# Seven products of quarters in the input projections of a state-space layer, and decay by rows

## The chip, the cores and the metric

The kernel runs on one core of a Trainium2 chip, as one launch. The metric is the device time of that core in microseconds (us), from the kernel's start to its end. Each kernel is run several times; the number to compare is the median. A profile comes from one further execution, whose time differs a little from the median.

## The reference

The model is a small stack on 1024 tokens of width 512: a mixture of experts, attention with 32 heads, the experts again, a linear layer with low-rank experts, a state-space (Mamba-2) layer, and the low-rank layer again. The change touches only the state-space layer. Cut to what matters, with `u` the normalized input (1024 x 512):

```python
proj = u @ in_proj_w.T                       # gate 4096, x 4096, B 1024, C 1024, dt 64
xBC  = silu(conv(hbc))                       # causal, 4 taps per column, plus a bias
dt_p = softplus(dt + dt_bias);  dA = exp(dt_p * A)
# 64 heads of 64 columns, 8 groups of 8 heads that share B and C (128 wide each)
state = state * dA_t + dtx_t * B_t           # per head 64 x 128, token by token
y_t   = state . C_t
y     = y + x * D
yn    = y * rsqrt(mean(y*y over the group) + EPS) * norm_weight * silu(gate)
out   = yn @ out_proj_w.T
```

Here `u @ in_proj_w.T` is the projection. The recurrence is computed in chunks of 128 tokens. Inside a chunk, y is a matrix product with a lower-triangular matrix of decays; what came before the chunk enters through the state at the chunk's start, decayed by a factor that depends on head and token alone.

## The kernel before, in words

All operands are fp32. Tokens lie on 8 tiles of 128. `hT` holds the normalized input transposed: 4 blocks of 128 rows, 1024 columns.

The function `mamba` walks over 16 **units**: 8 groups of heads, each in two halves of 512 tokens. A unit has 4 chunks of 128 tokens, and 5 **pairs** of projected blocks of 128 columns: pair 0 is B and C, pairs 1 and 2 are x, pairs 3 and 4 are the gate. For each chunk, the loop at the end of `mamba` calls `scan` for the running unit, `project_pair` for the next unit (two pairs in the first chunk, one in each other), `prepare` for the next chunk, and `project_out` for this one. A list scheduler in the framework then fixes the order in which the instructions stand on each engine; each engine works its own queue in that order, and semaphores join them. In the built program before the change, the order on TensorE is close to the written one.

- **`project_pair`** fills two PSUM banks (`ps_in`, pool `pbig`) through `project`: for each of two blocks, 4 matmuls of 128x512 (L230). For B, C and x, `conv_silu` then lets ScalarE read the bank with scale and bias (L1157), VectorE add three shifted taps from the same bank (L1161) and, in the second half, patch the first columns from `hist`, the last three columns of the first half (L1170). A Silu follows (L1180). `xd` is x scaled by D for a whole unit (L1224). For the gate, one Silu reads both banks (L1204).
- **`prepare`** loads two rows of decays per head from DRAM, each spread over 128 partitions (`dd`, SyncE's queue, L1259). VectorE turns the first into the triangular matrix `e` (L1265, L1273), and GpSimd multiplies the second with C into `cs` (L1290). Transposes (`ps_tr`, L156) and VectorE give `xdt` (L1278); GpSimd gives `xw` (L1284).
- **`scan`** computes y in one bank (`ps_y`, L1308): 8 matmuls of `xdt` with `e`, 8 of the old state with `cs`. VectorE adds `xd` (L1317), ScalarE squares (L1321), VectorE multiplies with the gate (L1323), and GpSimd adds four blocks of squares in two steps (L1340, L1341). `ps_st` (L1326) and two additions carry the state on (L1333, L1336).
- **`project_out`** sums the squares over partitions (`ps_ss`, L1349), gets the root on VectorE and GpSimd (L149, L150), multiplies with the output weights (`ps_out`, L1360) and adds to `x` (L1363).
- **`load_group`** loads four weight tiles per group on SyncE's queue, into the four buffers of `wpool`, and scales the output weights on ScalarE (L1146).

Other stages already use seven products: `products`, called at L884 and L912, and `sums` (L636), which builds the sums of weights on GpSimd.

## Time and profile before

| What | Value |
|---|---|
| median of 3 runs | 2933.5 us (2931.63 to 2933.84) |
| the profiled execution's own time | 2935.3 us |
| its span, first to last instruction | 2933.6 us |
| TensorE busy (PE) | 2800.9 us, 95% |
| VectorE busy (DVE) | 1745.8 us, 60% |
| ScalarE busy (ACT) | 709.4 us, 24% |
| GpSimd busy (POOL) | 898.8 us, 31% |
| mean granted TensorE clock | 0.978 |

PE is TensorE, PEld its weight loads, which overlap with matmuls; DVE is VectorE, ACT ScalarE, POOL GpSimd, SP SyncE. A line such as L230 is a line of the kernel's file, often that of a helper that many callers share, so the names of the tiles (`ps_in<-hT,w_x`) say which use is meant. A fp32 matmul shows as two passes, so a count of 512 stands for 256 calls. Buffers' numbers are left out of names.

### The profile page before, as it was taken

To read this page: it belongs to the slowest core of one execution; us is meant where nothing else is said; L and a number is where in the kernel's file an instruction comes from. 1 tells how busy PE (TensorE), PEld (TensorE's weight loads), DVE (VectorE), ACT (ScalarE), POOL (GpSimd) and SP (SyncE) were. 2 spreads that over 40 slices of the span, in tenths; PEclk is the share of its full clock that TensorE was granted. 3 is DMA by queue.
4 is the path that set the end of the run, shared out by engine and by line. 5 is a ranking of instruction groups with operands and counts; after the bars stand their busy time and mean duration, and the time that the engine had idled before them with its cause. 6 is when DMAs were issued, how large, how long until landed. Compare 5 with 4: busy or idle time off the path is not lost.

```text
span 2933.6 us, 30294 instructions
## 1 busy us (share of the span) xinstructions
PE 2800.9 (95%) x11051; PEld 1587.3 (54%) x11051; DVE 1745.8 (60%) x3239; ACT 709.4 (24%) x1381; POOL 898.8 (31%) x733
## 2 busy tenths in 40 slices
PE   5979999999999999999999769899999999999989
PEld 3435666656666666666654334454555555555544
DVE  3146555665656656556564234777776777767673
ACT  1212212231212222212222222422222232222320
POOL 4231112121122212112100230255554545455450
PEclk8989999999999999999999889999999999999999
DMA  8420001010010001001015340233232222223210
GB/s 297 126 72 29 15 15 44 1 44 15 15 44 15 29 15 43 15 15 43 1 36 194 101 122 18 83 101 108 86 108 94 86 98 97 93 87 122 87 44 29
DMA packets 102178, 196.99 MB, mean 67 GB/s; under 512 B 9040, under 2 KB 34800, under 8 KB 102032
## 3 DMA queue, kind: packets, MB, share of 16 engines
q1 hardware_dynamic: 84896, 157.15, 16.1%
q0 software_dynamic: 6240, 20.45, 2.7%
q10 hardware_dynamic: 10896, 17.47, 1.6%
q8 instruction: 89, 1.46, 0.2%
q14 instruction: 57, 0.47, 0.1%
HBM read 176.17 MB, written 18.87 MB: 66 GB/s over the span
## 4 chain that ended last, share of the span: by engine, by line
PE 84%; DVE 6%; POOL 4%; issue 3%; DMA 2%; ACT 0%; POOLq 0%; DVEq 0%; SPq 0%; ACTq 0%
PE ps_in L230 15%; PE ps_m L912 13%; PE ps_o L732 8%; PE ps_s L708 8%; PE ps_tr L156 7%; PE ps_out L1360 6%; PE ps_m L884 6%; PE ps_wo L821 6%; PE ps_e L510 5%; PE ps_y L1308 3%; PE ps_up L241 2%; PE ps_st L1326 1%; DVE xc L1161 1%; DVE e_seg L1265 1%; PE ps_v L241 1%
## 5 line engine op out<-in xcount | busy, mean ns | idle before, releaser
L708 PE MATMUL ps_s<-kT,qT 128*128 128x512 f32 (+3 forms) x768 | 292.8, 488 | 0.1
L732 PE MATMUL ps_o<-pT,v 128*128 128x512 f32 (+3 forms) x768 | 260.4, 489 | 0.0
L753 ACT COPY pT<-ps_tr 128x256 f32<-128x256 f32 (+2 forms) x192 | 91.7, 478 | 647.3 <-PE ps_tr L156 635.5
L722 ACT ACTIVATE pr<-ps_s,nm 128x128 f32<-128x128 f32 (+7 forms) x256 | 190.3, 744 | 238.3 <-DVE nm L719 207.9
L1360 PE MATMUL ps_out<-w_out,yg 128*128 128x512 f32 x512 | 241.1, 615 | 3.0 <-DVE yg L1323 3.0
L230 PE MATMUL ps_in<-hT,w_g 128*128 128x512 f32 x512 | 227.1, 596 | 8.2 <-issue 8.2
L1290 POOL TENSOR_TENSOR cs<-cT,dd 128x1024 f32<-128x1024 f32 x56 | 184.2, 3289 | 161.6 <-PE ps_y L1308 138.8
L230 PE MATMUL ps_in<-hT,w_x 128*128 128x512 f32 x512 | 225.8, 593 | 0.0
L732 PEld LDWEIGHTS ps_o<-pT,v 128*128 128x128 f32 x768 | 144.3, 191 | 145.6 <-issue 99.9
L719 DVE TENSOR_REDUCE nm<-ps_s 128x1 f32<-128x128 f32 (+7 forms) x256 | 192.2, 752 | 3.9
L156 PEld LDWEIGHTS ps_tr<-ident,pr 128*128 128x128 f32 x1152 | 136.9, 142 | 76.1 <-issue 44.8
L156 PE MATMUL ps_tr<-ident,pr 128*128 128x128 f32 x1152 | 171.4, 276 | 4.5 <-DVE pr L724 3.2
L510 PE MATMUL ps_e<-w_all,xt_s 128*128 (+1 forms) x368 | 168.1, 601 | 0.0
L724 DVE TENSOR_SCALAR pr<-pr,sm 128x128 f32<-128x128 f32 (+7 forms) x256 | 162.9, 637 | 7.7 <-DVE sm L723 0.5
L230 PEld LDWEIGHTS ps_in<-hT,w_g 128*128 128x128 f32 x512 | 96.6, 190 | 127.8 <-issue 127.8
L230 PEld LDWEIGHTS ps_in<-hT,w_x 128*128 128x128 f32 x512 | 97.0, 190 | 120.9 <-issue 120.4
L1265 DVE TENSOR_TENSOR_SCAN e_seg<-dd,eye 128x1024 f32<-128x1024 f32 x64 | 152.3, 2380 | 7.7 <-PE ps_y L1308 5.8
L1161 DVE SCALAR_TENSOR_TENSOR xc<-ps_in,conv,xc 128x511 f32<-128x511 f32 (+2 forms) x192 | 141.5, 737 | 17.9 <-ACT xc L1157 17.6
L708 PEld LDWEIGHTS ps_s<-kT,qT 128*128 128x128 f32 x768 | 127.5, 192 | 39.8 <-issue 26.8
L1360 PEld LDWEIGHTS ps_out<-w_out,yg 128*128 128x128 f32 x512 | 94.5, 195 | 98.4 <-issue 98.4
L806 POOL TENSOR_TENSOR so<-oT 128x256 f32<-128x256 f32 x28 | 20.0, 726 | 380.2 <-DVE oT L739 336.7
L1284 POOL TENSOR_TENSOR xw<-xdt,erev 128x512 f32<-128x512 f32 x56 | 58.4, 1043 | 251.6 <-DVE xdt L1278 195.0
(271 smaller groups left out, 4759.2 us busy)
## 6 DMA issues: line engine op xcount, KB each, us to landing
dd<-decay SPq DMA_DIRECT2D x128, 512.0 KB
w_all<-in_w_e_dram SPq DMA_DIRECT2D x16, 1024.0 KB
outs<-y_e ACTq DMA_DIRECT2D x46, 256.0 KB
w_v<-in_wkv_dram SPq DMA_DIRECT2D x8, 1024.0 KB
w_q<-in_wq_dram SPq DMA_DIRECT2D x32, 256.0 KB
w_k<-in_wkv_dram SPq DMA_DIRECT2D x8, 1024.0 KB
w_o<-in_wo_dram SPq DMA_DIRECT2D x8, 1024.0 KB
w_x<-in_in_wt_dram SPq DMA_DIRECT2D x8, 1024.0 KB
```

Source lines behind the costliest of these rows:

```text
L156: nc.tensor.transpose(ps[:, i * P : (i + 1) * P], src(i), ident)
L230: nc.tensor.matmul(ps[:, cols : cols + n], lhsT=w[:, k, c0 : c0 + P], rhs=hT[:, k, t0 : t0 + n], start=(k == 0), stop=(k == KT - 1),)
L510: nc.tensor.matmul(ps, lhsT=xt[:, k, :], rhs=w_all[:, bass.ds(ep, 1), k, :].rearrange("p e c -> p (e c)"), start=(k == 0), stop=(k == KT - 1),
L708: nc.tensor.matmul(ps[:, j : j + m], lhsT=qT[:, qt * P : (qt + 1) * P], rhs=kT[:, j : j + m], start=True, stop=True,)
L719: nc.vector.tensor_reduce(nm, ps[:, :n], AX.X, ALU.max, negate=True)
L722: nc.scalar.activation(pr[:, :n], ps[:, :n], AF.Exp, bias=nm, accum_out=sm)
L732: nc.tensor.matmul(ps[:, lo:512], lhsT=v[:, kb, hh * P : (hh + 1) * P], rhs=pT[:, kb, lo:512], start=(kb == 0), stop=(kb == last),)
L821: nc.tensor.matmul(ps[:, j, :], lhsT=lf[i][k][:, j * P : (j + 1) * P], rhs=rt[i][:, k, :], start=(first and j == 0 and k == 0), stop=(k == 1),
L912: nc.tensor.matmul(ps, lhsT=gr["left"][i][:, k, hh * P : (hh + 1) * P], rhs=right[i][:, k, :], start=(first and k == 0), stop=(last and k ...
L1265: nc.vector.tensor_tensor_scan(e.rearrange("p h l -> p (h l)"), dd[:, 0, :], eye8.rearrange("p h l -> p (h l)"), 0.0, ALU.mult, ALU.add,)
L1290: nc.gpsimd.tensor_tensor(cs, un["cT"][:, tok].unsqueeze(1).to_broadcast([P, HPG, P]), dd[:, 1, :].rearrange("p (h l) -> p h l", l=P), ALU ...
L1360: nc.tensor.matmul(po, lhsT=yg[:, k, :], rhs=w_o[:, k, :], start=(k == 0), stop=(k == 3))
```

## The change

It has four parts.

- **Projections as seven products.** Weights and input are cut into quarters (rows and columns halved). `quarter` makes four differences of `hT`'s quarters once per half on VectorE, one of them in place. `left_bc` and `left_in` make four sums of the weights' quarters per weight tile on GpSimd, one in place. `project_pair` becomes a generator with four steps: bank `pa` collects products 1, 6, 7 and 4, and ScalarE copies its content out (`snap`) before each next one; `pb` holds product 2 and `pc` products 5 and 3, in a second bank. VectorE adds three of the four results, ScalarE copies the fourth.
- **The convolution reads SBUF.** Results go to `raw`, which has three columns of history in front; the three taps are then full width, and the patches from `hist` are gone. `conv_both` runs one chunk later.
- **State's part of y decayed by rows.** `ps_z` is the old state times C: 4 matmuls of 128x128. VectorE multiplies it with the decays `ec`, which are loaded onto the two halves of the partitions; GpSimd adds `xd`; y is then `ps_y` plus that. `cs` is gone. `xd` is made per chunk, 4 pieces of 128 columns.
- **Buffers and loads.** `dd` is turned into `e` in place; `xdt`, `xw`, `xd`, `z`, `y`, `sq` and `yg` have one buffer each. The four weight loads of a group are spread over the chunks of two units.

The diff, cut to its core:

```diff
+                def quarter(hf):
+
+                    q1, q2 = (slice(hf * 512 + i * 256, hf * 512 + (i + 1) * 256) for i in range(2))
+                    b11, b12 = hT[:, :2, q1], hT[:, :2, q2]
+                    b21, b22 = hT[:, 2:, q1], hT[:, 2:, q2]
+                    t1, t2, t4 = (tt[:, hf, i, :, :] for i in range(3))
+                    nc.vector.tensor_tensor(t1, b12, b11, ALU.subtract)
+                    nc.vector.tensor_tensor(t2, b22, t1, ALU.subtract)
+                    nc.vector.tensor_tensor(t4, b21, t2, ALU.subtract)
+                    nc.vector.tensor_tensor(b12, b22, b12, ALU.subtract)
+                    quarters.append({1: b11, 2: b21, 3: b22, 4: t4, 5: t1, 6: t2, 7: b12})
...
+            def left_in(gr, n):
+                w, ss = gr["w_" + n], par.sums[n]
+                gr["l_" + n] = sums(
...
+            def conv_silu(raw, ct, dst):
...
                 for s in (1, 2, 3):
                     nc.vector.scalar_tensor_tensor(
-                        dst[:, s:],
-                        ps[:, : half - s],
+                        dst,
+                        raw[:, 3 - s : 3 - s + half],
...
+            def project_pair(un, j, convs):
...
+                snap = sn.tile([P, 4, n], F32, tag="snap", name="snap")
+                mm(pa, 1, True)
+                nc.scalar.copy(snap[:, 0, :], pa)
+                mm(pb, 2, True)
+                yield
+                mm(pa, 6)
+                nc.scalar.copy(snap[:, 1, :], pa)
+                mm(pc, 5)
+                nc.scalar.copy(snap[:, 3, :], pc)
+                yield
...
+                mm(pa, 7)
+                nc.scalar.copy(snap[:, 2, :], pa)
+                nc.vector.tensor_tensor(d1[:, :n], pb, snap[:, 0, :], ALU.add)
+                nc.vector.tensor_tensor(d2[:, n:], snap[:, 3, :], snap[:, 2, :], ALU.add)
+                yield
+                mm(pc, 3)
+                nc.vector.tensor_tensor(d1[:, n:], pc, snap[:, 1, :], ALU.add)
+                mm(pa, 4)
+                if gate:
+                    nc.scalar.activation(d2[:, n:], d2[:, n:], AF.Silu)
+                    nc.scalar.activation(d2[:, :n], pa, AF.Silu)
+                    nc.scalar.activation(d1, d1, AF.Silu)
                     return
+                nc.scalar.copy(d2[:, :n], pa)
...
+                e = ep.tile([P, HPG, P], F32, tag="dd", name="dd")
+                dd = e.rearrange("p h l -> p (h l)")
...
+                xd = w1.tile([P, 4, P], F32, tag="xd", name="xd")
+                for k in range(4):
+                    nc.scalar.activation(
+                        xd[:, k, :],
+                        un["xc"][:, k, tok],
...
-                    cs = ep.tile([P, HPG, P], F32, tag="cs", name="cs")
...
+                    pz = psml.tile([P, 512], F32, tag="ps", name="ps_z")
+                    for k in range(4):
                         nc.tensor.matmul(
+                            pz[:, k * P : (k + 1) * P],
+                            lhsT=before[:, k * P : (k + 1) * P],
+                            rhs=un["cT"][:, tok],
...
+                    z = w1.tile([P, 4, P], F32, tag="z", name="z_m")
+                    nc.vector.tensor_tensor(
+                        z, pz.rearrange("p (k l) -> p k l", l=P), ec, ALU.mult
+                    )
+                    nc.gpsimd.tensor_tensor(z, z, more, ALU.add)
+                    more = z
...
                 for i in range(4):
+                    pairs, early = [], convs
+                    convs = []
+                    if nxt is not None:
+                        pairs = [project_pair(nxt, j, convs) for j in plan[i]]
+                    go_on(pairs)
                     done = scan(un, i, *ready)
-                    if nxt is not None:
-                        for j in plan[i]:
-                            project_pair(nxt, j)
-                        if i == 1:
-                            finish_bc(nxt)
+                    go_on(pairs)
+                    for f in early:
+                        f()
...
+                    go_on(pairs)
+                    if un["gr"].pop("scale_o", False):
+                        scale_o(un["gr"])
                     project_out(*done)
+                    go_on(pairs)
```

## The prediction

> **What bounds the kernel now.** I first read the page's chain of work that ended last, to see which engine sets the end.
>
> ```profile
> PE 84%; DVE 6%; POOL 4%; issue 3%; DMA 2%; ACT 0%; POOLq 0%; DVEq 0%; SPq 0%; ACTq 0%
> PE ps_in L230 15%; PE ps_m L912 13%; PE ps_o L732 8%; PE ps_s L708 8%; PE ps_tr L156 7%; PE ps_out L1360 6%; PE ps_m L884 6%; PE ps_wo L821 6%; PE ps_e L510 5%; PE ps_y L1308 3%; PE ps_up L241 2%; PE ps_st L1326 1%; DVE xc L1161 1%; DVE e_seg L1265 1%; PE ps_v L241 1%
> ```
>
> TensorE sets it, and the products that the change rewrites (ps_in, L230) are its largest single piece. Next the busy time by stretch (columns: stretch, its length, then busy us of PE, PEld, DVE, ACT, POOL, then the granted clock).
>
> ```profile
> 1840.00:1860.00 20.00, 11.79 (x26) 5.67 (x26) 18.40 (x27) 12.51 (x16) 6.77 (x2) 0.83 0.39 135
> 2308.00:2376.00 68.00, 68.00 (x320) 35.72 (x315) 48.51 (x61) 16.17 (x24) 35.55 (x23) 1.00 0.23 78
> ```
>
> In the state-space stage (from 1876 us to about 2840 us) TensorE is busy for all 68.00 of 68 us: it waits for nobody. DVE has 29% free, POOL 48%. So the stage is as long as its matmuls, and a cut there counts in full, but every wait put on TensorE counts in full too. The first line, from the lead-in, shows a clock of 0.83 where TensorE idled (L230 after one idle of 8.2 us). Then one chunk in order of time (columns: start, duration, engine, line).
>
> ```profile
> 2230.37 1.09 PE L1308 MATMUL ps_y<-e_seg,xdt 128*64 128x128 f32 x16
> 2231.30 1.04 PE L1308 MATMUL ps_y<-cs,state 128*64 128x128 f32 x16
> 2232.27 1.13 PE L1326 MATMUL ps_st<-xw,btok 128*128 128x512 f32 x2
> 2233.23 7.03 PE L230 MATMUL ps_in<-hT,w_g 128*128 128x512 f32 x16
> 2234.72 0.68 DVE L1317 TENSOR_TENSOR y_m<-ps_y,xd 128x512 f32<-128x512 f32 x1
> 2235.49 0.63 ACT L1321 ACTIVATE sq<-y_m 128x512 f32<-128x512 f32 x1 [4.36 <-DVE y_m L1317]
> 2236.27 1.18 POOL L1340 TENSOR_TENSOR sq<-sq 128x256 f32<-128x256 f32 x1
> 2237.38 1.21 DVE L1273 TENSOR_TENSOR e_seg<-e_seg,gt 128x1024 f32<-128x1024 f32 x1
> 2237.53 1.38 POOL L1341 TENSOR_TENSOR sq<-sq 128x128 f32<-128x128 f32 x1
> 2240.10 0.60 PE L156 MATMUL ps_tr<-ident,xc 128*128 128x128 f32 x4
> 2240.54 0.28 PE L1349 MATMUL ps_ss<-ones,sq 128*128 128x1 f32 x2
> 2240.68 3.68 PE L1360 MATMUL ps_out<-w_out,yg 128*128 128x512 f32 x8
> 2244.29 1.09 PE L1308 MATMUL ps_y<-e_seg,xdt 128*64 128x128 f32 x16
> ```
>
> This is the cover that decides the case. ps_y is complete at 2232.3; the sum of squares needs it through y_m, sq and two POOL additions, which end at 2238.9; TensorE asks for it (ps_ss) at 2240.5. The 6.87 us of ps_in between them hide the whole chain, with 1.6 us to spare. The chunk takes 2244.29 - 2230.37 = 13.92 us. The chain of waits repeats every 127.2 us (POOL ss L150 at 2041.04 and 2168.19): two units of four chunks.
>
> **The change, part by part.**
>
> *Projections.* A fp32 matmul runs as two passes. Now: 16 passes of 512 columns take 6.87 us, 0.43 each. After: 7 products x 2 halves x 2 passes = 28 passes of 256 columns. The attention stage has such passes:
>
> ```profile
> 1378.81 1.89 PE L884 MATMUL ps_m<-w_v,tt 128*128 128x256 f32 x8
> 1380.53 1.89 PE L884 MATMUL ps_m<-sv,tt 128*128 128x256 f32 x8
> ```
>
> Eight start within 1.72 us: 0.216 each, so 28 take 6.04. Saved: 0.83 x 80 pairs = 66 us.
>
> *State's part of y.* Sixteen half-width passes (2231.30 to 2232.27, 0.97 us) become eight of 128x128; the eight ps_bc passes take 0.89. Saved: 0.08 x 56 = 4 us. With both, TensorE's work falls by 70 us: about 118 us per two units, if nothing waits.
>
> *ACT.* Added: 240 snapshots and 48 raw copies of 128x256 at 0.37 (pT of that shape), 107 us; the gate's one Silu (1.02) becomes three (about 1.5), 15; xd in 256 pieces of 128 columns, for which no row exists: between 0.27 (a plain copy, 128 columns) and 0.40 (that plus the 0.14 by which the scaled 512-column xd, 0.72, exceeds a plain copy, 0.58); I take 0.40, its own kind, so 102 for 46. About +180 us on an engine that is 24% busy: hidden as busy time. As a queue it isn't, see below.
>
> *DVE.* Goes: 144 patches from history (48 us) and the hist copies (7). Comes: 240 additions of 128x256 at about 0.39 (94), 56 z products at 0.68 (38), eight quarter differences (5). Net +82 us, within DVE's free 29%.
>
> *POOL.* Goes: cs, 184 us. Comes: z += xd, 56 x 1.27 = 71, and the weight sums, per group eight of 128x512 at 1.27 and four of 128x256 at 0.73 = 13.1, times 8 = 105. Busy time even; but cs was work that nobody waited for soon, and its replacements stand in TensorE's way.
>
> *SP and DMA.* 128 broadcasts of 512 KB become 64, and 112 of 128 KB. DVE's wait for dd was 1.9 us in all, so nothing is gained. SP issues 48 more, at 0.42. dd is now overwritten in place and its next load waits for ps_y of two chunks back, a chunk ahead of its use: about zero, at most a few us. The weight loads are spread over two units; w_out still lands some 5.6 us after its issue, then ACT scales it: hidden behind the first chunk's products as now.
>
> *The waits added, which decide.* In the order in which the changed program's instructions stand, three things are new.
>
> (a) ps_ss. After the last ps_z TensorE has ps_st (0.96), a transpose group (0.44) and 12, 6, 6 or 8 calls of 0.43 (plus ps_bc and bT, 1.3, in the third chunk): 6.6, 4.0, 5.3, 4.9 us. The chain is z 0.68, POOL add 1.27, y 0.68, sq 0.63, POOL 0.72 and 0.45 at their shortest, 4.8 with six hand-overs of 0.06; at mean durations (1.63 and 0.96 for the last two) 6.2. The old cover was 8.3 us for a chain of two links fewer.
>
> (b) POOL's queue. z_m's addition stands behind four sums of w_bc (2.9 us) once a group, and the sq addition amid four sums of w_x (5.1 us) and of w_g.
>
> (c) ACT's queue. xd now has one buffer, so its first piece waits until POOL has added the old one to z; behind it stand the snapshots for which the collecting bank, and so TensorE, waits. A worked chunk, from its first ps_y: ps_z ends at 3.2, z at 4.1, POOL is at the w_bc sums until 6.6, a short memset, the addition ends 8.05, xd takes ACT to 8.4, the snapshot ends at 8.8, and TensorE, idle since 5.7, goes on at 9.0 with its weights loaded: 3.2 us lost. y then ends at 8.8, sq at 9.7, POOL at 11.6, ps_ss comes at 11.7 instead of 10.3: 1.4 lost.
>
> I laid eight chunks out so, each instruction starting when its engine is free and its releaser done, durations from rows. Lost on products / on ps_ss, in us: 3.5/1.0, 4.3/1.4, 0.7/3.3, 5.3/3.3, 1.8/6.7, 1.3/1.4, 2.1/0, 1.7/3.2. That is 20.7 + 20.3 = 41 us per two units: 118 + 41 = 159 against 127.2. The same layout of the old order gives 126, so it is not biased against waits.
>
> *A rule against the change.* Rows first (shortest/median/longest, ns):
>
> ```profile
> L1323 DVE TENSOR_TENSOR yg<-y_m,sg x64: 674/991/1525, 1880.6 to 2895.6; 128x512 f32<-128x512 f32 x64
> L1161 DVE SCALAR_TENSOR_TENSOR xc<-ps_in,conv,xc x192: 648/736/750, 1842.4 to 2805.1; 128x511 f32<-128x511 f32 x64, 128x510 f32<-128x510 f32 x64, 128x509 f32<-128x509 f32 x64
> L1340 POOL TENSOR_TENSOR sq<-sq x60: 722/1702/2707, 1879.3 to 2824.3; 128x256 f32<-128x256 f32 x60
> ```
>
> The Trainium skill (SBUF — State Buffer, Who interferes with whom) says that a DVE instruction with two SBUF inputs and a GpSimd instruction that reads SBUF exclude each other for a whole instruction, while one SBUF input is free of it. The rows agree: yg (two SBUF inputs) and sq stretch, the convolution (PSUM and SBUF) doesn't; above, the second POOL addition ends with e_seg's 1.21. The change makes all 288 convolution steps read raw from SBUF. By rows at their shortest (0.65 instead of 0.74) that gains 26 us of DVE and the layout loses only 26 us per two units; by the rule, which stretches POOL's part of (a) and (b), 41. I take four fifths of the way to the rule.
>
> *Sum.* 15 units with projections, 7.5 pairs of units. By the rule 7.5 x 32 = 238, without it 7.5 x (118 + 26 - 127) = 130; at four fifths 216. Another page of the Trainium skill, TensorE: Matmul & The Clock Gate (Why this matters for your kernels), warns of idle gaps over about 3 us, after which the clock falls to half; around the 8.2 us gap the first stretch above lost 0.17 x 20 = 3.4 us of clock. Only the 6.7 us gap (once per two units) is likely to: by the layout's row zero, by the rule up to 25; I take 6. Lead-in and tail even out: the first products start before POOL has its sums, and the last unit has none. So +222 on the profiled execution's 2935.3 (span 2933.6 and 1.7 around it); the median of the runs, 2933.5, lies 1.8 lower. 3155.
>
> **The rivals.**
>
> *The waits bite, the port hardly does* (25%): 2933.5 + 130 = 3064. For it: cs, the longest POOL partner (3.29 us), is gone. Against: its place is taken by sums of 1.27, and the DVE steps with two SBUF inputs more than double (192 now, 288 + 80 added).
>
> *Worse* (12%): the clock falls in most long gaps and POOL's sums stretch each other: 3155 + 25 + 60 = 3240.
>
> *Faster* (5%): other work fills the waits. TensorE's place for it is the product of the next pair, put between. It would be 2933.5 - 70 = 2864. It decides if the loss stays under 70/15 = 4.7 us a unit, 1.2 a chunk; the worked chunk loses 4.6, and (a) alone, at shortest durations, 0.8 in the second chunk. I see nothing in the rows that shortens the two POOL links.
>
> *The products don't get cheaper* (3%): 28 passes equal 16 at 0.245 each; the row says 0.216. It adds up to 66 us.
>
> **How the numbers follow.** The case worked out has 55%: 3155, own range 3100 to 3215. With the others, the 8-in-10 range is 3040 to 3240; below it lie "faster" and the mildest of the first rival, above it half of "worse". Within 0.2% (6 us, about what a measurement can tell from no change): 1%. Faster 5%, slower 94%.
>
> **What would show it.** TensorE's busy share in the stage falls from 100% to 75-80%, with ps_ss waiting on POOL sq some 60 to 150 us in all and ps_in waiting on ACT snap and DVE; two units take near 155 us; ps_in's busy time falls by some 60 us; ACT's wait of xd on POOL z_m is among the longest; the convolution's DVE steps spread instead of sitting at 0.74. It is wrong if two units take under 127 us, or if TensorE's waits come mainly from a DMA.

## The result, and the profile after

The changed kernel takes 3191.7 us (median, 3187.92 to 3198.01) against 2933.7 us for the kernel before on the same chip: the ratio is 1.0884, with a 95% interval of 1.0869 to 1.0899. It is 258 us slower. The prediction was 3155 (range 3040 to 3240).

First the chain of work that ended last, of the changed kernel's page.

```profile
PE 73%; POOL 12%; DVE 8%; DMA 3%; issue 3%; ACT 1%; SPq 0%; POOLq 0%; DVEq 0%; ACTq 0%
PE ps_m L914 12%; PE ps_in L1268 9%; PE ps_o L734 8%; PE ps_s L710 7%; PE ps_out L1479 6%; PE ps_m L886 5%; PE ps_wo L823 5%; PE ps_tr L156 5%; PE ps_e L510 4%; PE ps_y L1410 2%; POOL z_m L1433 2%; PE ps_up L241 2%; POOL sq L1459 2%; PE ps_z L1422 2%; DVE xc L1233 1%
```

TensorE's share of the chain fell from 84% to 73%, and GpSimd's rose from 4% to 12%: `z_m` and `sq`, two additions on GpSimd, now stand in the chain themselves. Next the busy time by stretch (columns as before the change: stretch, its length, busy us of PE, PEld, DVE, ACT, POOL, granted clock, DMA share, GB/s).

```profile
2228.70:2389.83 161.13, 137.59 (x615) 91.30 (x614) 106.68 (x140) 55.86 (x140) 71.68 (x63) 0.94 0.20 61
2246.00:2251.20 5.20, 5.20 (x10) 2.20 (x10) 5.17 (x5) 0.46 (x2) 5.20 (x3) 0.67 0.01 3
```

The first line is two units: 161.13 us where they took 127.2, with TensorE idle for 23.5 of them and a granted clock of 0.94 where it was 1.00. The second is explained below. Then one chunk in order of time (start, duration, engine, line, with the idle time before it and its releaser in brackets).

```profile
2237.08 1.16 PE L1422 MATMUL ps_z<-cT,state 128*128 128x128 f32 x8
...
2238.31 0.68 DVE L1430 TENSOR_TENSOR z_m<-ps_z,ec 128x512 f32<-128x512 f32 x1
...
2239.14 1.27 POOL L1433 TENSOR_TENSOR z_m<-z_m,xd 128x512 f32<-128x512 f32 x1 [6.65 <-DVE z_m L1430]
...
2240.45 0.69 DVE L1436 TENSOR_TENSOR y_m<-ps_y,z_m 128x512 f32<-128x512 f32 x1 [0.62 <-POOL z_m L1433]
2241.22 0.63 ACT L1440 ACTIVATE sq<-y_m 128x512 f32<-128x512 f32 x1
...
2242.20 0.95 POOL L1459 TENSOR_TENSOR sq<-sq 128x256 f32<-128x256 f32 x1
...
2242.72 1.03 PE L1268 MATMUL ps_in<-hT,w_g 128*128 128x256 f32 x4
2243.12 1.71 POOL L638 TENSOR_TENSOR s_x<-w_x 128x512 f32<-128x512 f32 x1
...
2244.79 0.90 POOL L1460 TENSOR_TENSOR sq<-sq 128x128 f32<-128x128 f32 x1
...
2245.74 0.38 PE L1468 MATMUL ps_ss<-ones,sq 128*128 128x1 f32 x2 [1.99 <-POOL sq L1460]
2245.99 5.38 PE L1479 MATMUL ps_out<-w_out,yg 128*128 128x512 f32 x8
```

The chain that the prediction named is there link by link, with one of the sums of weights (`s_x`) between GpSimd's two additions of squares. It ends 1.99 us after TensorE has nothing left to do. And then the next work, the same eight passes of `ps_out` that took 3.68 us in the kernel before, takes 5.38: that is the stretch with the granted clock of 0.67. Such a wait is paid twice, once as idle time and once as a clock at half speed afterwards. The waits of the changed kernel (engine, line waited for: us in total, times, longest) name the same places:

```profile
ACT xd L1388 <- POOL z_m L1433: 151.4, 48, 6.4
PEld ps_ss L1468 <- POOL sq L1460: 135.3, 52, 5.8
PE ps_ss L1468 <- POOL sq L1460: 114.9, 43, 5.4
POOL raw L1297 <- DVE bT L1233: 96.9, 8, 22.5
PE ps_in L1268 <- ACT snap L1283: 33.0, 37, 2.2
```

**A ledger of TensorE.** For every kernel I took 48 chunks of the stage, from the fifth to the fifty-third start of `ps_out`, in the view in order of time, and split the time of two units into three: *idle* (TensorE had nothing to start), *clock* (half of the working time inside stretches at half clock, since passes that start 0.43 us apart elsewhere start 0.85 apart in them), and *work* (the rest: from the start of one group of passes to the start of the next, at full clock).

| us in two units | total | idle at ps_ss | idle at ps_in | clock | work |
|---|---|---|---|---|---|
| before | 127.1 | 0.6 | 0 | 0 | 126.5 |
| changed | 162.3 | 16.0 | 7.8 | 10.2 | 128.3 |

The difference, 35.2 us, times the 7.5 pairs of units is 264 us, against 258 measured, so the whole loss lies in this stage. The last column is the surprise: TensorE's own work did not get less at all. In the changed kernel 280 passes of `ps_in` take 66.7 us at full clock, 0.238 each, where 160 took 68.8; 128 passes of `ps_y` take 11.4 us, 0.089 each instead of 0.060, and 56 of `ps_z` take 7.0. Four rows of the chunk above show where the price comes from:

```profile
2235.22 1.13 PE L1268 MATMUL ps_in<-tt_m,w_x 128*128 128x256 f32 x4
2236.28 0.87 PE L1410 MATMUL ps_y<-dd,xdt 128*64 128x128 f32 x10
...
2238.94 1.03 PE L1268 MATMUL ps_in<-tt_m,s_g 128*128 128x256 f32 x4
2239.80 0.60 PE L156 MATMUL ps_tr<-ident,bT 128*128 128x128 f32 x4
```

From the start of one row to the start of the next, four passes between two groups of `ps_y` take 1.06 us, four in front of a transpose 0.86, which is 0.216 each. Over the 48 chunks, at full clock, each of 102 passes in front of `ps_y` takes 0.31 us to the next start, and each of the 54 that start right behind it takes 0.32; the 78 in front of transposes, `ps_z` and `ps_out` take 0.216. Of the 6.2 us that 280 passes take above 0.216 each, 2.6 lie beside `ps_y` and 3.2 beside a wait.

### The profile page after: what moved, and what is told of

It reads as the page before. It is cut to its first block, busy times and chain, and to the rows that moved or that the text cites. A ratio compares the mean times of both kernels' runs of the same rounds, so it can differ in the third digit from the quotient of the medians.

```text
span 3190.0 us, 32210 instructions
## 1 busy us (share of the span) xinstructions
PE 2883.1 (90%) x11563; PEld 1795.4 (56%) x11563; DVE 1855.6 (58%) x3351; ACT 875.6 (27%) x2095; POOL 949.1 (30%) x877
## 3 DMA queue, kind: packets, MB, share of 16 engines
q1 hardware_dynamic: 106144, 138.28, 13.4%
## 4 chain that ended last, share of the span: by engine, by line
PE 73%; POOL 12%; DVE 8%; DMA 3%; issue 3%; ACT 1%; SPq 0%; POOLq 0%; DVEq 0%; ACTq 0%
PE ps_m L914 12%; PE ps_in L1268 9%; PE ps_o L734 8%; PE ps_s L710 7%; PE ps_out L1479 6%; PE ps_m L886 5%; PE ps_wo L823 5%; PE ps_tr L156 5%; PE ps_e L510 4%; PE ps_y L1410 2%; POOL z_m L1433 2%; PE ps_up L241 2%; POOL sq L1459 2%; PE ps_z L1422 2%; DVE xc L1233 1%
## 5 line engine op out<-in xcount | busy, mean ns | idle before, releaser
L1479 PE MATMUL ps_out<-w_out,yg 128*128 128x512 f32 x512 | 302.6, 739 | 0.0
L1370 DVE TENSOR_TENSOR_SCAN dd<-dd,eye 128x1024 f32<-128x1024 f32 x64 | 181.3, 2833 | 13.3 <-DMA dd<-decay 13.2
L1479 PEld LDWEIGHTS ps_out<-w_out,yg 128*128 128x128 f32 x512 | 116.8, 240 | 121.8 <-issue 120.7
L1433 POOL TENSOR_TENSOR z_m<-z_m,xd 128x512 f32<-128x512 f32 x56 | 73.7, 1315 | 354.4 <-DVE z_m L1430 278.6
L1233 DVE SCALAR_TENSOR_TENSOR xc<-raw,conv,xc 128x512 f32<-128x512 f32 x192 | 164.1, 856 | 14.3 <-ACT xc L1225 13.0
L710 PEld LDWEIGHTS ps_s<-kT,qT 128*128 128x128 f32 x768 | 127.5, 192 | 39.8 <-issue 26.8
L1468 PE MATMUL ps_ss<-ones,sq 128*128 128x1 f32 x152 | 30.5, 281 | 127.3 <-POOL sq L1460 114.9
L1388 ACT ACTIVATE xd<-xc,dsk 128x128 f32<-128x128 f32 x256 | 93.0, 396 | 152.5 <-POOL z_m L1433 151.4
L661 POOL TENSOR_SCALAR w_q<-w_q 128x1024 f32<-128x1024 f32 x16 | 44.3, 2770 | 289.2 <-DMA w_q<-in_wq_dram 288.6
L518 DVE TENSOR_TENSOR y_e<-ps_e,b_all 128x512 f32<-128x512 f32 x46 | 31.8, 692 | 169.0 <-PE ps_e L510 165.5
L1482 DVE SCALAR_TENSOR_TENSOR x<-ps_out,ss,x 128x512 f32<-128x512 f32 x64 | 47.8, 746 | 136.1 <-PE ps_out L1479 119.1
```

The lines of the kernel that those rows point to most:

```text
L710: nc.tensor.matmul(ps[:, j : j + m], lhsT=qT[:, qt * P : (qt + 1) * P], rhs=kT[:, j : j + m], start=True, stop=True,)
L1233: nc.vector.scalar_tensor_tensor(dst, raw[:, 3 - s : 3 - s + half], conv[:, ct, 3 - s : 4 - s], dst, ALU.mult, ALU.add,)
L1370: nc.vector.tensor_tensor_scan(dd, dd, eye8.rearrange("p h l -> p (h l)"), 0.0, ALU.mult, ALU.add,)
L1479: nc.tensor.matmul(po, lhsT=yg[:, k, :], rhs=w_o[:, k, :], start=(k == 0), stop=(k == 3))
```

## The experiments

All times are medians; ratios are against the kernel before on the same chip, with 95% intervals. The ledger's lines are worked out in the same way for each.

**The two parts of the change apart.** The first run makes only the second part of the change, in the kernel before:

```diff
-                terms = [(xdt, e)] + ([(before, cs)] if before is not None else [])
...
+                more = un["xd"][:, :, tok]
+                if before is not None:
+                    pz = psml.tile([P, 512], F32, tag="ps", name="ps_z")
...
+                    nc.gpsimd.tensor_tensor(z, z, more, ALU.add)
```

> The kernel before with one part of the change alone: the state's part of y decayed by rows (ps_z, ec, z on VectorE, its addition of xd on GpSimd), cs gone, the projections as before. Theory of the waits in order: the projections of 6.9 us still stand between ps_y and ps_ss, and they covered the old chain with 1.6 us to spare; the new one is 2.1 us longer, so the cover is short by some 0.5 us in a chunk at mean durations: TensorE's work is even (ps_z's eight passes take 1.0 us, as much as the sixteen that go), and the time rises by 0 to 28 us: about 2945. Rival, in which the two parts of the change cost alike: above 3000. Rival, in which cs was what stretched VectorE's and GpSimd's instructions: below 2930.

Measured: 2944.3 us, ratio 1.0035 (1.0022 to 1.0048), as the theory of the waits said. Two units take 127.5, with 126.7 of work and 0.8 of idle time. Its waits at `ps_ss`:

```profile
PE ps_ss L1363 <- ACT sq L1335: 12.6, 4, 3.8
PE ps_ss L1363 <- POOL sq L1355: 6.7, 9, 0.8
```

So the longer chain alone hardly ever shows: 6.7 us in all on GpSimd's additions. The first line is the last unit, which has no products to stand between. The run also shows that the decay by rows saves TensorE nothing: in two units the 56 passes of `ps_z` take 7.0 us, and `ps_y` falls by 6.1 (14.3 to 8.2).

The second run is the changed kernel with that part put back:

```diff
+                terms = [(xdt, e)] + ([(before, cs)] if before is not None else [])
...
-                    z = w1.tile([P, 4, P], F32, tag="z", name="z_m")
...
-                    nc.gpsimd.tensor_tensor(z, z, more, ALU.add)
```

> The changed kernel with the state's part put back: cs on GpSimd again (made in place in its own load), sixteen passes of cs with the state collected into ps_y, y is ps_y plus xd; no ps_z, no z. The seven products stay. Theory of the waits in order: the chain before ps_ss loses z and GpSimd's addition (2.1 us), and xd no longer waits for GpSimd; but cs (2.3 us and up) stands in GpSimd's queue again, amid the sums of the weights. The waits that ACT's snapshots and VectorE's additions put on ps_in stay, as do most gaps in front of ps_ss: 3120 to 3185, about 3160. Rival, in which the parts simply add up: 3192 less what the rows alone add to the kernel before, so 3165 to 3192. Rival, in which the decay by rows is the main cause: below 3020.

Measured: 3112.3 us, ratio 1.0613 (1.0595 to 1.0630). This is below what I expected; the parts do not add up. The decay by rows costs 11 us alone, and 79 us (3191.7 less 3112.3) when it stands beside the rest of the change. The ledger: 125.0 of work, 7.7 idle at `ps_ss`, 12.9 at `ps_in`, 6.4 of clock. What is shorter is the wait at `ps_ss`, whose chain lost two links; at `ps_in` TensorE waits more than in the changed kernel.

**The place of the products.** The change also spreads a pair's products over four places of the chunk, ahead of `scan`, behind it, behind `prepare` and behind `project_out`, where the old kernel had all of them behind `scan`. One run takes that alone into the kernel before:

```diff
+                    go_on(pairs)
                     done = scan(un, i, *ready)
-                    if nxt is not None:
-                        for j in plan[i]:
-                            project_pair(nxt, j)
...
+                    go_on(pairs)
...
+                    go_on(pairs)
                     project_out(*done)
+                    go_on(pairs)
```

> The kernel before with one thing alone taken from the change: the sixteen passes of a pair spread over four places of the chunk (ahead of scan, after it, after prepare, after project_out) instead of all after scan. Nothing else differs: convolution from the bank, cs on GpSimd, two buffers. Theory of the cover: half of the 6.9 us of products leave the stretch between ps_y and ps_ss, the chain y, sq and GpSimd's two additions (4.4 us and more, with cs in GpSimd's queue) is then longer than what is left (4.9 us at best), and TensorE waits at ps_ss, with half-clock stretches behind the longer gaps: 2980 to 3040, about 3015. Rival, in which the single buffers, the SBUF convolution and the decay by rows made the 160 us that were left with the products undone: below 2950.

Measured: 3081.8 us, ratio 1.0514 (1.0496 to 1.0532): 151 us slower, with no seven products, no snapshots, no sums, no `z`. The rival is out, and my own figure was too low. The ledger: 127.6 of work, 8.1 idle at `ps_ss`, 6.2 at `ps_in`, 4.9 of clock. TensorE in order of time, two chunks of this run:

```profile
2213.31 3.60 PE L1203 MATMUL ps_in<-hT,w_g 128*128 128x512 f32 x8
2220.85 0.46 PE L1365 MATMUL ps_ss<-ones,sq 128*128 128x1 f32 x2 [3.94 <-POOL sq L1357]
2221.17 5.29 PE L1376 MATMUL ps_out<-w_out,yg 128*128 128x512 f32 x8
...
2233.12 1.88 PE L1203 MATMUL ps_in<-hT,w_g 128*128 128x512 f32 x4
2236.29 0.38 PE L1365 MATMUL ps_ss<-ones,sq 128*128 128x1 f32 x2 [1.28 <-POOL sq L1357]
2236.53 3.68 PE L1376 MATMUL ps_out<-w_out,yg 128*128 128x512 f32 x8
2240.05 1.88 PE L1203 MATMUL ps_in<-hT,w_g 128*128 128x512 f32 x4
```

The four passes at 2240.05 are work that used to stand ahead of `ps_ss`. They are not lost, but they come after the wait that they used to fill. The gap of 3.94 us is followed by a `ps_out` of 5.29, the gap of 1.28 by one of 3.68. What I had left out is `ps_in`'s own wait, 46 us in all on VectorE's convolution of the pair in hand (24.7 for `cT`, 21.5 behind `hist`), and most of the clock.

Two runs undo the seven products in the changed kernel, one with the new place of the products and one with the old:

```diff
-                mm(pa, 1, True)
-                nc.scalar.copy(snap[:, 0, :], pa)
-                mm(pb, 2, True)
+                mm(0, (0, 1))
                 yield
```

> The changed kernel with the seven products alone undone: sixteen passes of 512 columns a pair again, spread over the same four places of a chunk, each bank copied to raw by ScalarE (the gate's Silu reads the bank), no snapshots, no VectorE additions, no sums of weights on GpSimd. The convolution from SBUF, the single buffers, the decay by rows and the order of the chunk stay. Theory of the waits in order: the collecting banks and the sums are the larger part, but not all: half of a chunk's products now stand outside the stretch between ps_y and ps_ss, so some of the waits of ps_ss stay: 12 to 16 us of waits and clock in two units, 3030 to 3075. Rival, in which the products with their copies and sums are all of it: 2940 to 2965, as with the rows alone. Rival, in which convolution from SBUF, buffers and order are the cause, and the products cost nothing: above 3120.

Measured: 3093.1 us, ratio 1.0534 (1.0509 to 1.0559), again above what I expected, on the side of the cover. The ledger: 127.6 of work, 13.4 idle at `ps_ss` and nothing at `ps_in`, 6.9 of clock. So with the seven products gone, 160 of the 258 us stay. The next run adds this edit to it:

```diff
+                    done = scan(un, i, *ready)
                     go_on(pairs)
-                    done = scan(un, i, *ready)
+                    go_on(pairs)
+                    go_on(pairs)
                     go_on(pairs)
...
-                    go_on(pairs)
                     if un["gr"].pop("scale_o", False):
                         scale_o(un["gr"])
                     project_out(*done)
-                    go_on(pairs)
```

> The kernel of the run 'plain' (seven products undone, the rest of the change kept) with the old place of the products: all sixteen passes of a pair after scan, ahead of prepare. Theory of the cover: 7.4 to 8.3 us stand between ps_z and ps_ss again, against a chain of 6.2 at mean durations; most of ps_ss's 113 us of waits and of the half-clock stretches behind them go: 2950 to 3010, about 2985. Rival, in which convolution from SBUF and single buffers are what makes GpSimd's and VectorE's links late: above 3050.

Measured: 3009.4 us, ratio 1.0262 (1.0245 to 1.0280), 84 us less than with the new place, at the upper end of the range. This kernel has the chain of the run `rows`, but not all of its products between `ps_z` and `ps_ss`, and still 7.7 us of idle time in two units at `ps_ss`. The list scheduler decides the built order, and in four of the eight chunks of two units it put four of a pair's sixteen passes behind the first of `ps_out`:

```profile
2231.49 5.31 PE L1243 MATMUL ps_in<-hT,w_x 128*128 128x512 f32 x12
2236.64 0.60 PE L156 MATMUL ps_tr<-ident,xc 128*128 128x128 f32 x4
2239.36 0.38 PE L1433 MATMUL ps_ss<-ones,sq 128*128 128x1 f32 x2 [2.11 <-POOL sq L1425]
2239.60 1.10 PE L1444 MATMUL ps_out<-w_out,yg 128*128 128x512 f32 x2
2240.54 1.88 PE L1243 MATMUL ps_in<-hT,w_x 128*128 128x512 f32 x4
```

All the idle time stands in these four chunks (2.1, 2.2, 2.0 and 1.4 us, where the four passes are 1.72); the other four have none. So I measured, over the same 48 chunks, the *cover* (TensorE's time from the end of `ps_z`, or of `ps_y` where there is no `ps_z`, to `ps_ss`, without its waits) and the *chain* (from the same end to the end of GpSimd's second addition):

| mean us of a chunk | before | rows | plain_o | spread | plain | changed |
|---|---|---|---|---|---|---|
| cover | 10.2 | 10.2 | 9.4 | 7.1 | 5.9 | 5.4 |
| chain | 6.9 | 7.5 | 7.2 | 6.7 | 7.0 | 7.6 |

The chain hardly differs between these kernels; the cover does. What else of the 65 us between this run and `rows` belongs to single buffers, to the convolution one chunk later or to `xd` by chunks was not separated.

The last run on the place makes the same edit in the changed kernel itself. Here too the scheduler follows it only in part: 73% of the passes of `ps_in` stand between `ps_z` and `ps_ss`, where the changed kernel has 44% and the kernel before all:

> The changed kernel with the old place of the products: the four steps of each pair one after the other behind scan, ahead of prepare; nothing else differs. Theory of the cover: ps_ss's waits shrink to half or less, but the snapshots now have only the products' own passes to hide behind, so ps_in waits more: 3100 to 3165, about 3140. Rival, in which the place of the products is all that matters: below 3060. Rival, in which the collecting banks need the spread: above 3192.

Measured: 3115.1 us, ratio 1.0621 (1.0603 to 1.0639): 77 us less than the changed kernel, inside the range. As expected the wait goes from one place to the other: idle at `ps_ss` 8.8 instead of 16.0, at `ps_in` 10.3 instead of 7.8; work 125.6 and clock 7.5.

**Links of the chain.** TensorE sums the four blocks of squares itself, so that GpSimd's two additions go:

```diff
                 n = 4
-                if not un["last"]:
+                if un is None:
                     nc.gpsimd.tensor_tensor(sq[:, :2, :], sq[:, :2, :], sq[:, 2:, :], ALU.add)
```

> The changed kernel without GpSimd's two additions of squares: TensorE sums the four blocks itself, eight passes of one column in place of two (some 0.7 us more of TensorE in a chunk). Theory of the waits in order: the two links (at least 1.2 us, 2.3 us with what stands between them in GpSimd's queue) were the end of the chain in front of ps_ss; in the two units from 2228.7 us seven gaps of 1.3 to 5.3 us stood there, 18 us in all, and most close. With the half-clock stretches that follow such gaps, 90 us go, less 40 us of passes where nothing covers them: 3080 to 3140, about 3100; ps_ss's waits fall from 135 us to under 50. Rival, in which the waits only move on, to ps_in: 3170 to 3200. Rival, in which the port between VectorE and GpSimd is the cause: above 3160, since z's addition, xw and the sums stay.

Measured: 3068.2 us, ratio 1.0459 (1.0441 to 1.0476). This takes 124 us off the changed kernel, more than expected, although TensorE's work rises to 131.6. Idle at `ps_ss` falls from 16.0 to 0.5 us, the clock's share from 10.2 to 3.1. Of the rival, in which the waits move on, only the rise from 7.8 to 10.3 at `ps_in` is left. The next run leaves the sums of weights out:

```diff
-            f() if later is None else later.append(f)
+            if pool is not None:
+                f() if later is None else later.append(f)
+        if pool is None:
+            s1, s2, s4 = a21, a12, a11
```

> The changed kernel without the sums of the weights' quarters in the state-space stage: GpSimd leaves them out, and TensorE multiplies plain quarters in their place, so the projections are not those of the reference; all else is the same. It takes 13 us of GpSimd's queue out of two units, out from between the links of the chain to ps_ss, and the port partner that lasts longest. Theory of the waits in order: about 11 us of two units go: 3080 to 3140, about 3105. Rival, in which the sums are hidden as busy time (GpSimd is 30% busy): 3175 to 3195. Rival, in which they are the whole cause of ps_ss's waits: below 3060, as with TensorE summing the squares.

Measured: 3093.3 us, ratio 1.0547 (1.0529 to 1.0565): inside the range. TensorE multiplies plain quarters in their place, in the same order. It is 98 us for what the prediction counted as 105 us of busy time, on an engine that the page shows 30% busy. Idle at `ps_ss` is 9.4, at `ps_in` 5.5, clock 4.7. GpSimd's first addition of squares has the same median with the sums and without (0.96 us), so they did not stretch it; VectorE's scan does get shorter (3.06 to 2.65), and how much of the gain that makes was not separated from their place in the queue. Then z's addition on VectorE:

```diff
-                    nc.gpsimd.tensor_tensor(z, z, more, ALU.add)
+                    nc.vector.tensor_tensor(z, z, more, ALU.add)
```

> The changed kernel with one addition moved: z plus xd on VectorE instead of GpSimd (0.68 instead of 1.27 us, no hand-over between z, its addition and y). It shortens the chain to ps_ss by some 0.7 us, takes it out from behind the sums of w_bc, and xd, which has one buffer, waits for VectorE instead of GpSimd. Theory of the waits in order: some 6 us of two units: 3110 to 3165, about 3145; ACT's wait of xd on GpSimd (149 us) is gone, and snap's hold on ps_in falls. Rival, in which ps_ss's last two links alone count: 3170 to 3190. Rival, in which VectorE, 0.68 us fuller in a chunk and in turn with GpSimd, is what is late: 3195 to 3230.

Measured: 3140.9 us, ratio 1.0707 (1.0678 to 1.0736), 51 us less, as expected. The waits of this run:

```profile
PE ps_ss L1468 <- POOL sq L1460: 129.8, 52, 6.4
...
PE ps_in L1268 <- DVE sg L1306: 3.8, 3, 1.4
...
PE ps_in L1268 <- ACT snap L1283: 2.6, 5, 0.7
```

The wait on `snap` is down from 33.0 to 2.6 us, and idle at `ps_in` from 7.8 to 1.3 in two units; `xd` itself waits 74 us, now on VectorE, instead of 151. So what held the snapshots was `xd`, at the head of ScalarE's queue, waiting for GpSimd's addition. The wait at `ps_ss` hardly moved (16.0 to 17.5): the two additions of squares and the sums among them are still there. This separates the prediction's (a) and (c).

**The clock.** Work that nobody needs, put where TensorE waits:

```diff
+                for _ in range(8):
+                    nc.tensor.matmul(
+                        pss[:, :P], lhsT=ident, rhs=ident, start=True, stop=True
+                    )
                 for k in range(n):
```

> The changed kernel with work added that nobody needs: in front of each ps_ss TensorE multiplies the identity by itself eight times (sixteen passes of 128 columns, about 1.9 us, 120 us in all), into the bank that ps_ss then overwrites. Theory that TensorE's half-clock stretches (20 us in the two units from 2228.7 us, about 150 us in the stage) follow gaps of about 1.7 us and more: the fillers lie in the gaps, four of the five stretches of two units go, and the granted clock of the stage rises to 0.97 or more; 6.8 us gained against some 3 us of fillers that find no gap: 3145 to 3190, about 3165, faster in spite of the added work. Rival, in which the clock follows something else (the load of the other engines, or the kind of matmul): the clock stays and only what finds no gap is added, 3200 to 3220; if the gaps don't hide the fillers either, 3310.

Measured: 3216.1 us, ratio 1.0968 (1.0950 to 1.0986). In time I was wrong: it is 24 us slower than the changed kernel, not 27 faster. In the clock I was right: the mean granted clock rises from 0.956 to 0.969, and the time at half clock after 1870 us falls from 174.5 to 92.9 us. In the ledger the clock's share is halved (10.2 to 5.0), but of 15.3 us of fillers in two units the gaps took up only 3.6. One chunk of this run shows why:

```profile
2249.88 1.74 POOL L638 TENSOR_TENSOR s_x<-w_x 128x512 f32<-128x512 f32 x1
2251.69 1.60 POOL L638 TENSOR_TENSOR s_x<-s_x,w_x 128x512 f32<-128x512 f32 x1
2252.08 3.35 DVE L1370 TENSOR_TENSOR_SCAN dd<-dd,eye 128x1024 f32<-128x1024 f32 x1
2252.61 1.95 PE L1468 MATMUL ps_ss<-ident 128*128 128x128 f32 x16
2253.25 2.70 POOL L1459 TENSOR_TENSOR sq<-sq 128x256 f32<-128x256 f32 x1
2255.92 1.26 POOL L638 TENSOR_TENSOR s_x<-w_x,s_x 128x512 f32<-128x512 f32 x1
2257.14 0.63 POOL L1460 TENSOR_TENSOR sq<-sq 128x128 f32<-128x128 f32 x1
...
2257.82 0.38 PE L1472 MATMUL ps_ss<-ones,sq 128*128 128x1 f32 x2 [3.26 <-POOL sq L1460]
2258.07 3.68 PE L1483 MATMUL ps_out<-w_out,yg 128*128 128x512 f32 x8
```

With the fillers in the program the list scheduler's order is another: two of the sums stand ahead of the first addition of squares, where none did in the chunk shown above. The addition then meets the scan, and the gap behind the filler is longer than that chunk's 1.99 us without it. So the run is no clean measure of what a filler costs. The last line is worth a look all the same: behind a gap of 3.26 us `ps_out` runs at full clock, while 1.99 us in the changed kernel were followed by half clock. The last section shows what makes the difference.

**The best version that the runs point to.** TensorE sums the squares, and z's addition and `xw` go to VectorE, first with the new place of the products:

```diff
-                if not un["last"]:
+                if un is None:
...
-                    nc.gpsimd.tensor_tensor(z, z, more, ALU.add)
+                    nc.vector.tensor_tensor(z, z, more, ALU.add)
...
-                    nc.gpsimd.tensor_tensor(
+                    nc.vector.tensor_tensor(
                         as_heads(xw), as_heads(xdt), per_head(erev, un, i), ALU.mult
```

> The changed kernel with three links taken off GpSimd: TensorE sums the squares' blocks itself, z plus xd and xw are made on VectorE. GpSimd keeps the sums of weights, the state's decay and the memsets. Theory of the waits in order: only waits of ps_in on snapshots and VectorE are left, some 15 us of two units, with 128 us of TensorE's own work at full clock and 5 us for the squares: 148 less what overlaps, 20 us less than the changed kernel: 3000 to 3045, about 3025, and not faster than the kernel before, since the work itself is no less than its 126.5. Rival, in which the savings add up: below 2990. Rival, in which VectorE becomes the bound: above 3065, no better than with the squares alone.

Measured: 3018.8 us, ratio 1.0297 (1.0280 to 1.0314), inside the range. And with the old place:

> The run 'n4_z_xw' (squares summed by TensorE, z plus xd and xw on VectorE) with the old place of the products as well, the best version that the runs point to. Theory of the waits in order: little of ps_ss's wait is left to cover there, so the old place gains little and costs waits on snapshots: 2990 to 3025, about 3010. Rival, in which uninterrupted passes get TensorE's work down (0.216 us a pass instead of 0.237, some 6 us of two units): 2960 to 2985. Faster than the kernel before only if waits and work both fall: below 2933.

Measured: 2987.5 us, ratio 1.0182 (1.0165 to 1.0199). This falls between my range (2990 to 3025) and that of the rival, in which the work gets less (2960 to 2985), and the work did fall: the passes of `ps_in` take 64.2 us, where they take 66.7 in the changed kernel. Two units take 134.6 us: 5.4 idle, 0.3 of clock, 129.0 of work, of which 6.6 are the sums of squares (1.3 in the kernel before). This is 204 us less than the changed kernel and still 56 more than the kernel before. With the squares' extra 5.3 us taken out, the work is 123.7: in this order, in which 71% of the passes stand between `ps_z` and `ps_ss` and others still among `ps_out` and `ps_y`, the seven products and the rows together are worth some 3 us of two units, and the waits and the sums of squares that come with them cost 11 (5.4 of idle time, 0.3 of clock, 5.3 of squares).

The runs side by side, in us of two units:

| run | time | total | idle at ps_ss | idle at ps_in | clock | work |
|---|---|---|---|---|---|---|
| before | 2933.7 | 127.1 | 0.6 | 0 | 0 | 126.5 |
| rows | 2944.3 | 127.5 | 0.8 | 0 | 0 | 126.7 |
| n4_z_xw_o | 2987.5 | 134.6 | 0.7 | 4.7 | 0.3 | 129.0 |
| plain_o | 3009.4 | 137.7 | 7.7 | 0 | 2.3 | 127.7 |
| spread | 3081.8 | 146.9 | 8.1 | 6.2 | 4.9 | 127.6 |
| plain | 3093.1 | 147.9 | 13.4 | 0 | 6.9 | 127.6 |
| seven_o | 3115.1 | 152.2 | 8.8 | 10.3 | 7.5 | 125.6 |
| changed | 3191.7 | 162.3 | 16.0 | 7.8 | 10.2 | 128.3 |

## Why the prediction was right in sign, and where its sum was wrong

The sum was 118 us of work, 38 of waits and 0.8 of clock in two units. The measured terms are 128.3, 23.8 and 10.2. The total came out 5 us of two units short, because three wrong terms nearly cancel: that 3155 lies so near 3191.7 is luck. (One product of the sum is also off: 7.5 x 17 is 127.5 and not 130, which moves the total by half a microsecond.)

- **"28 take 6.04", and "TensorE's work falls by 70 us": the step that failed.** A pass takes 0.238 us in this stage, not the 0.216 that I read from an unbroken run of eight; the rival that the products don't get cheaper, which breaks even at 0.245, had 3% and came close to the truth. The 0.216 holds inside a group here too; what I left out are the passes beside `ps_y` and beside a wait. `ps_y`'s own passes went from 0.060 to 0.089, since groups of products now stand among them: in `rows` they take 0.064, in `seven_o` 0.072. The Trainium skill (TensorEngine Tiling (Array Packing), Key Properties) says that a change of tiling mode drains TensorE; `ps_y` is the one product of the chunk with 64 output rows, and the starts fit that, since borders with the other products cost almost nothing; that the extra 0.1 us is a drain no run here shows. The saving of 4 us by `ps_z` was not there either (7.0 us in two units for the 6.1 that went).
- **(a), the chain to ps_ss: right, and the main cause.** I had 20.3 us for it in two units; 16.0 were measured, and `n4`, which shortens this chain alone, brings it to 0.5. That the cover shrinks because products move out from between was in the step ("6.6, 4.0, 5.3, 4.9", a mean of 5.2, against 8.3), and it is 5.4 in the changed kernel; the chain, for which the step adds two links, grew by only 0.7 us (6.9 to 7.6), so the lost cover is the larger part. What the step didn't say is that this is a third change beside the two in the title, and dear by itself: 151 us in the kernel before, where the decay by rows costs 11.
- **(b), GpSimd's queue: right.** Without the sums 98 us go, on an engine that is 30% busy.
- **(c), ScalarE's queue: the mechanism right, the size not.** `xd`'s wait on GpSimd (151.4 us) does hold the snapshots, and `zdve` frees them; but TensorE lost 7.8 us there in two units, not 20.7. Which of the layout's instructions stood too late was not settled.
- **The port.** I expected the convolution's steps to spread, because they read `raw` from SBUF. They hardly did (shortest, median, longest in ns; the first row is of the kernel before, the others of the changed one):

```profile
L1265 DVE TENSOR_TENSOR_SCAN e_seg<-dd,eye x64: 2273/2282/3128, 1839.6 to 2854.1; 128x1024 f32<-128x1024 f32 x64
...
L1233 DVE SCALAR_TENSOR_TENSOR xc<-raw,conv,xc x192: 718/748/1279, 1841.3 to 3055.2; 128x512 f32<-128x512 f32 x192
...
L1370 DVE TENSOR_TENSOR_SCAN dd<-dd,eye x64: 2271/3056/3282, 1852.5 to 3110.4; 128x1024 f32<-128x1024 f32 x64
...
L1459 POOL TENSOR_TENSOR sq<-sq x60: 715/957/2702, 1875.6 to 3071.0; 128x256 f32<-128x256 f32 x60
```

  The instruction that got slower is the scan, with two operands in SBUF: its median is 3.06 us, where it was 2.28. GpSimd's first addition, on the chain to `ps_ss`, got faster (0.96, where it was 1.70): the additions of squares were held up less than before, not more. The convolution's median is 0.01 above what it was on PSUM. The rule in the prediction (SBUF — State Buffer, Who interferes with whom) fits what is seen, but I had picked the wrong partner, and with it four fifths of the way from 26 to 41 us of waits; 23.8 were measured. (In the prediction's rows the second addition ends 0.32 us behind `e_seg`'s product, not with it.)
- **The clock: the mechanism right, its size more than tenfold too small.** I took 6 us in all, for one gap of over 3 us in two units. Measured are 10.2 us in two units, 77 in 15 units: the clock falls after much shorter gaps than the rule that I used says (next section but one).
- **What would show it.** TensorE's share is 85% (137.59 of 161.13), not 75 to 80, because slow and broken passes count as busy; `ps_ss`'s wait of 114.9 us lies in the range of 60 to 150; two units take 161 instead of 155; `xd`'s wait is among the longest; `ps_in`'s work falls by 2.1 us of two units, 16 us in all instead of 60.

## What to carry to other kernels

A product that needs fewer passes pays only if the passes keep their price in the place where they will stand, so read the price from a stretch with as many interruptions. When TensorE sets the end, a move of its work within a stage is a change of its own: write down what stood between each producer and its consumer before and after, and read it from the built program: the same edit in the source put 90% of the passes back in one kernel and 73% in another. And an engine that is 30% busy can still be what everyone waits for, if what it does stands in the order in which it must be done.

## What the runs showed of the hardware that was not expected

TensorE's clock falls after short gaps. Over the 14 kernels traced here, I set each gap of TensorE above 0.9 us, from 1870 us to the fifty-third start of `ps_out`, beside the clock record, and counted those in which, or within 2.2 us of whose end, a stretch of half clock (3.4 us long, or two or three times that) begins:

| gap, us | 0.9 to 1.5 | 1.5 to 2.0 | 2.0 to 3.0 | 3.0 to 3.4 | over 3.4 |
|---|---|---|---|---|---|
| gaps | 135 | 49 | 108 | 84 | 47 |
| followed by half clock | 0 | 19 | 64 | 76 | 47 |

The shortest gap so followed was 1.55 us, the longest that was not 3.29 us, and no stretch of half clock in this part of the stage stood without a gap. The Trainium skill (TensorE: Matmul & The Clock Gate, Why this matters for your kernels) warns of gaps over about 3 us; in these runs a gap of half that can be enough.

What decides in between can be read from the same record. In each of the 14 traces, the starts of half clock after the first 100 us lie on one grid of 3.413 us, to within 1 ns. Cut at its ticks, the windows that ran at full clock show this:

| TensorE idle in the window | up to 45% | 45 to 60% | over 60% |
|---|---|---|---|
| windows | 3427 | 109 | 157 |
| half clock from the window's end | 2 | 46 | 157 |

So it is not the gap's length that counts, but how much of one window is idle, with an edge near half. In the changed kernel the gap of 1.99 us lies whole in the window from 2242.63 to 2246.04, and half clock begins at 2246.04. In the run `fill` a tick at 2256.25 cuts the 3.26 us into 1.69 and 1.58, each a little under half of 3.413, and nothing follows. In the changed kernel this makes a gap of 1.99 us cost 3.7 (1.99 of idle time, and 1.70 by which `ps_out` is longer).
